# A GPTQ feed-forward behind a Mamba scan: the zero-subtracted integers of gate and up are unpacked a second time, after the scan

## The chip, the cores and the metric

The kernel runs on one core of one Trainium2 chip. The core has TensorE (PE; its weight loads are shown as PEld), VectorE (DVE), ScalarE (ACT), GpSimd (POOL) and SyncE (SP), which here only issues DMA transfers. The transfers run on 16 DMA engines. The metric is the device time of one execution in microseconds (us), taken as the median of some runs. The profile comes from one execution that was recorded by the hardware profiler.

## The reference

Two layers work on a state `x` of 2 batches, 512 tokens and 512 channels. Each of the four blocks is `x = x + layernorm(block(layernorm(x)))`. The first block is a Mamba block with a state of 16 per channel. The second, which the change is about, is a gated feed-forward with 4-bit GPTQ weights:

```python
def dequant_gptq(qweight, scales, zeros, groupsize):     # 8 nibbles along K in each int32
    q = qweight[k // PACK, :] >> (k % PACK * 4)[:, None] & 15
    z = zeros[:, n // PACK] >> (n % PACK * 4)[None, :] & 15
    s = scales.astype(jnp.float32)
    zp = (z.astype(jnp.float32) + 1.0) * s
    return q.astype(jnp.float32) * s[g] - zp[g]          # g = k // 128
...
gate = x2 @ Wg        # 512 -> 1376
up = x2 @ Wu          # 512 -> 1376
inter = gate * jax.nn.sigmoid(gate) * up
out = (inter @ Wd).astype(jnp.float16)
```

The third block is a small attention over 16 head channels, the fourth a feed-forward with a router; neither is touched.

## The kernel before

**Two forms of the same weights.** Gate and up have 512 rows and 1376 columns each. A packed word of a row of `gate_q` or `up_q` holds eight rows of the weight. One *word step* takes nibble `j` of every word of a stretch of columns, for gate and up at once (128 partitions: 64 of each), and gives 128 rows by up to 512 columns. There are three stretches (`CUTS`): 512, 512 and 352 columns, so 24 steps in all. Two results of a step are stored in DRAM: the integer less its zero point, `q - (z + 1)`, in `wgi_d`, and the same times the scale in `wgu_d`. Batch 0 multiplies with the scaled weights (`gu_weights(0, j)` reads `wgu_d`). Batch 1 multiplies with the integers (`gu_weights(1, j)` reads `wgi_d`), with its activations split into a high and a low part (`hhl`), and applies the scales (`gus`) as it takes the sums out of PSUM.

**A step in detail** (`GateUpWords.steps`, L278 to L315). `nibble` (L237, DVE) shifts and masks into a buffer `q`. Then the zero is subtracted into the same buffer, seen as float (`wi`): by DVE in one instruction (L292), or, where the step is given to GpSimd, by an ACT copy (L295) and a GpSimd subtraction (L299). SP stores `wi` to `wgi_d` (L303). GpSimd multiplies `wi` with the scale into another buffer `w` (L307), and stores that to `wgu_d` (L312; on GpSimd's queue in the head, on SP's in the scan). There are four buffers `q` and four `w` in the head, and four tiles of another pool stand in for `w` in the last four steps there. The integers' store walks the DRAM tensor in the order of its 4 groups of rows, then 32 rows in each:

```python
nc.sync.dma_start(
    out=wgi_d[j * RG : (j + 1) * RG, :, :, n0:n1].rearrange("r a k n -> k r a n"),
    in_=wi[:, :n],
)
```

**The stages.** *The head* (to 85.3 us, where the first scan instruction starts): batch 0 is normalised and transposed, then eight channel tiles of the Mamba input are projected (PE, `px`, L626), taken out with a bias (`evict_x`, ACT, L479), convolved (`conv`, three DVE instructions, L486) and put through `silu` (ACT, L640); two channels later their rank projection runs (PE, `psm`, L500). The word steps of the first two stretches are written between these channels: four at channel 0, then one per channel on DVE, two more on GpSimd's route at channel 2 and one more at channels 4 and 6, and the sixteenth after the ranks. After the ranks come their norm (`ranks_norm`, L507), a transpose (`pt`, L540), `dt`, and the loads of the broadcast rows B and C (L561). *The scan* (85.3 to 589 us) runs 128 steps of DVE multiply, DVE scan (L1108), GpSimd multiply (L1114) and PE sum (L1136), with the projections of batch 1 and batch 0's gate and up as side work; the eight steps of the third stretch are placed there (`words_job`, L1065). *Behind the scan* (590 to 659 us) PE does batch 1's Mamba output (`po`, L1309) and batch 0's down projection (`fo`, L1328), while `down_words` unpacks the down weights (DVE, GpSimd, SP) and `normed_job` normalises and transposes batch 1 (`tp_f`, L1285) into `hhl`. *Batch 1's gate, up and down* (`gptq(1)`, 659 to 755 us) follow: PE's `fg`, `fu` (L1450), taken out by ACT (L1432), DVE (L1436) and GpSimd (L1440), beside batch 0's attention. The rest (755 us on) is batch 1's attention and the last block.

**What sets the order.** Instructions of PE, ACT, DVE and GpSimd stand on their engines in the order in which they are traced (`pin`, L407). Side work is made of generators: `spawn` starts one after a lag, each `yield n` lets n ticks pass, and behind the scan there is one tick for each `po` or `fo` matmul of the source. DMA issues on SP are not pinned; they stand in an order that the tile scheduler decides, and SP works through them one by one, so an issue that waits for its data or its buffer holds up the issues behind it. Weights of gate, up, `wo` and `wd0` share three buffers (`wst`).

Of the kernel before, what the change touches and what calls it, by code (L numbers as in the profile page):

```python
# [57 lines left out]
def tile_sandwich(  # L58
# [157 lines left out]
    def word_loads(parts, n0, n1, qw, z, s, step, eng, engz):  # L216

        def at(p0, m):
            return slice(p0, p0 + step * (m - 1) + 1, step)

        n = n1 - n0
        for p0, src, r0, r1, sc, zd in parts:
            eng.dma_start(out=qw[at(p0, r1 - r0), :n], in_=src[r0:r1, n0:n1])
        for rows_, dst, en in ((4, s, eng), (5, z, engz)):
            for part in parts:
                p0, r0, r1, rows = part[0], part[2], part[3], part[rows_]
                g0, g1 = r0 // RG, r1 // RG
                for ga, gb, m in ((g0, g1, RG), (g1, g1 + 1, r1 - g1 * RG)):
                    if m:
                        q0 = p0 + step * (ga * RG - r0)  # L230
                        en.dma_start(
                            out=dst[at(q0, (gb - ga) * m), :n],
                            in_=rows[ga:gb, n0:n1].unsqueeze(1).to_broadcast([gb - ga, m, n]),
                        )
# [4 lines left out]
    class GateUpWords:  # L239
# [38 lines left out]
        def steps(self, eng=nc.vector):  # L278
            n0, n1, qw, z, s, q_, w_, j = self.todo.pop(0)
            n, nm = n1 - n0, f"gu{n0}_{j}"  # L280
            q = q_(nm)
            beside = bool(scans)
            if beside:
                eng = nc.gpsimd

            while beside and (now[0] % 2 == 0 or pool_at[0] == (now[0] - 1) // 2 - 1):
                yield 1
            nibble(q[:, :n], qw[:, :n], j)
            yield 2
            w, wi = w_(nm), q.bitcast(F32)  # L290
            if eng is nc.vector:
                eng.tensor_sub(wi[:, :n], q[:, :n], z[:, :n])  # L292
                yield 2
            else:
                nc.scalar.copy(wi[:, :n], q[:, :n])  # L295
                yield 2
                if beside:
                    yield from pool_turn()
                eng.tensor_sub(wi[:, :n], wi[:, :n], z[:, :n])  # L299
                yield 1  # L300
                if beside:
                    yield from pool_turn()
            nc.sync.dma_start(  # L303
                out=wgi_d[j * RG : (j + 1) * RG, :, :, n0:n1].rearrange("r a k n -> k r a n"),
                in_=wi[:, :n],
            )
            nc.gpsimd.tensor_mul(w[:, :n], wi[:, :n], s[:, :n])  # L307
            if beside:
                yield 2
            hp_ = KH * RG  # L310
            rows = slice(j % 2 * hp_, (j % 2 + 1) * hp_)
            (nc.sync if beside else nc.gpsimd).dma_start(  # L312
                out=wgu_d[rows, :, j // 2, n0:n1].rearrange("r a n -> (r a) n"), in_=w[:, :n]
            )
            yield 2  # L315
# [20 lines left out]
    def down_words(d, dq, loaded):  # L336

        nr = INTER // PACK
        m, hw = nr - P, H // 2
        qw, z, s, r, n = loaded  # L340
        wd_v = wd_d.rearrange("(r e) n -> e r n", e=PACK)
        for j in range(PACK):
            q = dq.tile([P, S], I32, tag="q", name=f"q_d{d}_{j}", bufs=2)
            nibble(q[:r, :n], qw[:r, :n], j)
            w = dq.tile([P, S], F32, tag="w", name=f"w_d{d}_{j}", bufs=3)
            nc.vector.tensor_sub(w[:r, :n], q[:r, :n], z[:r, :n])
            nc.gpsimd.tensor_mul(w[:r, :n], w[:r, :n], s[:r, :n])
            if d == 0:
                nc.sync.dma_start(out=wd_v[j, :P, :], in_=w[:, :H])
            else:  # L350
                for a in range(2):
                    nc.sync.dma_start(out=wd_v[j, P:nr, ts(a, hw)], in_=w[a * m : (a + 1) * m, :hw])
            yield 2 - j % 2

    def head_sums(dq):

# [71 lines left out]
    with ExitStack() as mamba:  # L428
# [786 lines left out]
        ps_x = pool(ctx, "px", 1, PSUM)  # L1215
        ps_tp = pool(ctx, "ptp", 1, PSUM)
        hlp = pool(ctx, "hl", side="right")
        hhl = [hlp.tile([P, KH, S], F32R, name=f"h{nm}1") for nm in ("hi", "lo")]

        def obank(name):  # L1220
# [30 lines left out]
        with ExitStack() as p3:  # L1251
            dq = pool(p3, "dq2", 1)

            def normed_job(i, ps):

                name = f"mo1_{i}"
                o = new_u(f"o1_{i}")
                nc.scalar.copy(o, ps)
                yield 3
                mv = moments([o], name)  # L1260
                rs = rstd(mv, name, 1)
                yield 2
                nm = minus_mean(mv, rs, name, 1)
                yield 1
                apply(o, o, rs, nm, 0)
                yield 2
                nc.vector.tensor_add(xs(1)[i], xs(1)[i], o)
                name = f"f1_{i}"
                mv = moments([xs(1)[i]], name)
                rs = rstd(mv, name, 1)  # L1270
                yield 2
                nm = minus_mean(mv, rs, name, 1)
                yield 1
                xn = jrow(f"xn_{name}")
                apply(
                    xn.rearrange("p (k j r) -> p k r j", k=KH, j=PACK),
                    xs(1)[i].rearrange("p (k r j) -> p k r j", k=KH, j=PACK), rs, nm, 0,
                )
                yield 2
                tps = []  # L1280

                def turn():
                    tp = bank(f"tp_f1_{i}").rearrange("p (k t) -> p k t", k=KH)
                    for kc in range(KH):
                        nc.tensor.transpose(tp[:, kc, :], xn[:, ts(kc, P)], ident)  # L1285
                    tps.append(tp)

                def split():
                    hi, lo = (t_[:, :, ts(i, P)] for t_ in hhl)
                    nc.scalar.copy(hi, tps[0])  # L1290
                    yield 1
                    nc.vector.tensor_sub(lo, tps[0], hi.bitcast(F32))

                asks.append((turn, split()))

            def words_jobs():
                yield from down_words(0, dq, down[0])
                yield from down_words(1, dq, down[1])
                yield 20
                yield from head_sums(dq)  # L1300

            def outs():
                po = [obank(f"po1_{i}") for i in range(TB)]
                for j in range(NCH // 2):
                    w = wo_pair(1, 0, j)
                    tiles = [(e, i) for e in range(2) for i in range(TB)]
                    for e, i in sorted(tiles, key=lambda ei: ei[j == NCH // 2 - 1]):
                        c = 2 * j + e
                        nc.tensor.matmul(  # L1309
                            po[i], g[1][c][:, ts(i, P)], w[:, e, :],  # L1310
                            start=(c == 0), stop=(c == NCH - 1),
                        )
                        yield
                        if c == NCH - 1:
                            spawn(normed_job(i, po[i]), 1)
                for i, m in enumerate(IC):
                    j, e = divmod(i, 2)
                    if not e:
                        w = wst.tile([P, 2, H], F32, tag="w4", name=f"wd0_{j}")
                        n = len(IC[i : i + 2])  # L1320
                        nc.sync.dma_start(
                            out=w[:m, :n],
                            in_=wd_d[i * P : i * P + n * m].rearrange("(k p) h -> p k h", p=m),
                        )
                    for t in range(TB):
                        if not i:
                            fo0.append(obank(f"fo0_{t}"))
                        nc.tensor.matmul(  # L1328
                            fo0[t], its[i][:m, ts(t, P)], w[:m, e],
                            start=(i == 0), stop=(i == len(IC) - 1),  # L1330
                        )
                        yield

            fo0 = []
            spawn(words_jobs(), 1)
            run(outs())
            while jobs or asks:
                if asks:
                    answer()
                tick()  # L1340
            pin()
# [304 lines left out]
    def chain(b, fo, ask):  # L1646
        yield from ffn_out(b, fo)
        yield from gptq_norm(b)
        yield from attention(b, ask)

    spawn(chain(0, fo0, lambda fn, then: asks.append((fn, then))), 1)
    run(gptq(1))
    while jobs or asks:
# [77 lines left out]
```

## Time and profile before

| | us |
|---|---|
| median of 3 runs | 925.68 (923.48 to 926.89) |
| the profiled execution | 925.2 |
| its span, first to last instruction | 923.4 |
| PE busy, whole span | 834.6 (90%) |
| DVE busy | 714.0 (77%) |
| POOL busy | 506.4 (55%) |
| ACT busy | 443.9 (48%) |

By stage (busy us of each engine, granted TensorE clock as a share of full speed, and the mean busy share of the 16 DMA engines):

| stage, us | PE | DVE | ACT | POOL | clock | DMA |
|---|---|---|---|---|---|---|
| head, 0 to 85.3 | 60.7 | 45.6 | 29.5 | 46.4 | 0.88 | 0.54 |
| scan, 85.3 to 589.9 | 457.8 | 482.4 | 315.1 | 389.6 | 0.96 | 0.25 |
| behind the scan, 589.9 to 659.1 | 69.2 | 36.6 | 13.1 | 20.5 | 0.97 | 0.52 |
| batch 1 gate, up, down, 659.1 to 755 | 91.2 | 72.4 | 54.3 | 33.8 | 1.00 | 0.30 |
| rest, 755 to 923.4 | 155.8 | 77.1 | 31.9 | 16.3 | 0.96 | 0.10 |

An engine that is busy for nearly all of a stage bounds it; where none is, the stage waits for something else, and the views of waits and of the timeline tell for what. The times of the stages are read off the first scan instruction, the first `po` and the first `fg` matmul. A busy PE is not PE at its peak, and matmul ends are modelled. Time in which an engine only issues a DMA is not counted as busy.

### The profile page before, as it was taken

Reading aid. Unit: us, or ns where it says so; the run is one execution under the profiler, and the core shown is the slowest. Engines: PE = TensorE matmul, PEld = TensorE weight load, DVE = VectorE, ACT = ScalarE, POOL = GpSimd, SP = SyncE. Lnnn points to the kernel's source line nnn. Section 1 sums busy time; section 2 is a strip of 40 time slices with the busy share of each in tenths; the row PEclk is TensorE's granted clock in tenths of the full one; section 3 lists DMA queues with packets and bytes.
Section 4 is the critical chain, followed back from the end, with each engine's and each line's share of the span. In section 5 each row is a group of like instructions: output and inputs, shape, how many; then the busy total and the mean of one; then the engine's idle time right before and its main releaser. Section 6 shows DMA issues by size and latency. Waiting matters only on the chain. (4 is left out here: it accounts for less than half of the span.)

```text
span 923.4 us, 7390 instructions
## 1 busy us (share of the span) xinstructions
PE 834.6 (90%) x2188; PEld 386.6 (42%) x2188; DVE 714.0 (77%) x835; ACT 443.9 (48%) x682; POOL 506.4 (55%) x354
## 2 busy tenths in 40 slices
PE   6678897987999989959999999799989999999995
PEld 3343333332354434324444443244446545545442
DVE  6545999999999999999999999665385964445226
ACT  3226787566567755564656555013345554310110
POOL 6642988776688778886778787541133420011001
PEclk9887999998999999999999999799999999999998
DMA  6654911111000494410110102364332231101001
GB/s 190 215 192 157 361 60 33 47 46 54 23 24 26 131 330 169 160 41 0 46 45 23 46 9 85 127 222 160 91 92 69 71 115 55 59 12 57 24 0 46
DMA packets 47130, 85.76 MB, mean 93 GB/s; under 512 B 8014, under 2 KB 22201, under 8 KB 47090
## 3 DMA queue, kind: packets, MB, share of 16 engines
q1 hardware_dynamic: 44818, 79.29, 25.5%
q0 software_dynamic: 1984, 5.47, 1.7%
q10 hardware_dynamic: 288, 0.52, 0.2%
q8 instruction: 17, 0.28, 0.1%
q14 instruction: 23, 0.19, 0.1%
HBM read 68.40 MB, written 16.88 MB: 92 GB/s over the span
## 5 line engine op out<-in xcount | busy, mean ns | idle before, releaser
L1114 POOL TENSOR_TENSOR bx<-bx,C 128x1024 f32<-128x1024 f32 x128 | 302.0, 2360 | 107.3 <-DVE bx L1108 79.7
L1108 DVE TENSOR_TENSOR_SCAN bx<-da,bx 128x1024 f32<-128x1024 f32 x128 | 291.5, 2278 | 0.0
L1136 PE MATMUL py<-bx,ident 128*128 128x512 f32 x480 | 236.5, 623 | 28.1 <-POOL bx L1114 24.4
L1088 ACT ACTIVATE da<-dt,A 128x511 f32<-128x511 f32 x256 | 176.6, 691 | 144.0 <-DVE bx L1108 139.1
L1104 DVE TENSOR_TENSOR bx<-du,B 128x1024 f32<-128x1024 f32 x127 | 152.9, 1204 | 5.2 <-ACT da L1088 2.8
L1136 PEld LDWEIGHTS py<-bx,ident 128*128 128x128 f32 x480 | 92.0, 198 | 154.8 <-issue 96.7
L130 POOL TENSOR_TENSOR rs_lo<-ve_lo,mhalf 128x1 f32<-128x1 f32 x8 | 7.0, 880 | 91.8 <-DVE ve_lo L128 91.8
L756 PE MATMUL pg<-xT,w_g 128*128 128x512 f32 x114 | 55.7, 619 | 1.1 <-ACT dt L574 1.1
L1571 PE MATMUL pup<-hT_l,wup 128*128 128x512 f32 x128 | 56.2, 593 | 0.0
L1635 PE MATMUL pd<-wdn,hid 128*128 128x512 f32 x128 | 55.6, 595 | 0.0
L1440 POOL TENSOR_TENSOR pg<-pg,pg 128x512 f32<-128x512 f32 (+1 forms) x11 | 15.3, 1391 | 59.0 <-DVE pg L1436 59.0
L1411 PE MATMUL fo<-wd,pg 128*128 128x512 f32 (+1 forms) x88 | 44.2, 593 | 0.1
L1028 PE MATMUL fg<-hT_f,wg 128*128 128x512 f32 (+1 forms) x88 | 42.5, 594 | 0.0
L1028 PE MATMUL fu<-hT_f,wu 128*128 128x512 f32 (+1 forms) x88 | 40.4, 594 | 1.4 <-ACT dt L574 1.4
L486 DVE SCALAR_TENSOR_TENSOR u<-px,ch,u 128x511 f32<-128x511 f32 (+2 forms) x48 | 35.8, 747 | 7.0 <-ACT u L479 5.9
L1328 PE MATMUL fo<-wd,it 128*128 128x512 f32 (+1 forms) x88 | 38.6, 592 | 0.0
L1635 PEld LDWEIGHTS pd<-wdn,hid 128*128 128x128 f32 x128 | 24.6, 192 | 31.4 <-issue 30.9
L1571 PEld LDWEIGHTS pup<-hT_l,wup 128*128 128x128 f32 x128 | 23.9, 190 | 28.2 <-issue 28.2
L1588 DVE TENSOR_TENSOR hid<-hid 128x512 f32<-128x512 f32 x16 | 11.0, 687 | 32.0 <-ACT hid L1587 32.0
L756 PEld LDWEIGHTS pg<-xT,w_g 128*128 128x128 f32 x114 | 22.1, 198 | 31.6 <-issue 28.4
L626 PE MATMUL px<-xT,w_x 128*128 128x512 f32 x64 | 33.3, 671 | 0.7 <-ACT xT L606 0.7
L1436 DVE SCALAR_TENSOR_TENSOR pg<-fg,gus,pg 128x512 f32<-128x512 f32 (+1 forms) x22 | 16.3, 742 | 21.0 <-ACT pg L1432 21.0
(253 smaller groups left out, 1262.8 us busy)
## 6 DMA issues: line engine op xcount, KB each, us to landing
wo<-in_W_outT SPq DMA_DIRECT2D x20, 512.0 KB
B<-scr SPq DMA_DIRECT2D x16, 512.0 KB
C<-scr SPq DMA_DIRECT2D x16, 512.0 KB
w_x<-in_W_in SPq DMA_DIRECT2D x8, 512.0 KB
wgi_d<-q_gu SPq DMA_DIRECT2D x16, 256.0 KB
wgu_d<-w_gu POOLq DMA_DIRECT2D x16, 256.0 KB, 6.2
w_g<-in_W_in SPq DMA_DIRECT2D x8, 512.0 KB
wup<-in_up_w SPq DMA_DIRECT2D x8, 512.0 KB
```

What stands on the lines that cost most here:

```text
L486: nc.vector.scalar_tensor_tensor(uc[:, s:], ps[:, : S - s], ch[:, c, KCONV - 1 - s : KCONV - s], uc[:, s:], ALU.mult, ALU.add,)
L756: nc.tensor.matmul(ps, w[:, k, ts(e, P)], xT[b][:, k, :], start=(k == 0), stop=(k == KH - 1))
L1028: nc.tensor.matmul(ps[:m], wt[j][a][:, kc, e * P : e * P + m], hT[:, kc, :], start=(kc == 0), stop=(kc == KH - 1),)
L1088: nc.scalar.activation(das[s % 2][:, i, 1:], st["dt", b, c][:, 1:], AF.Exp, scale=A[:, c, n : n + 1])
L1104: nc.vector.tensor_mul(bx, st["du"].unsqueeze(1).to_broadcast([P, NG, S]), Bbs[b][gi])
L1108: nc.vector.tensor_tensor_scan(flat, das[s % 2].rearrange("p n t -> p (n t)"), flat, 0.0, ALU.mult, ALU.add)
L1114: nc.gpsimd.tensor_mul(bxs[s], bxs[s], Cbs[b][s % NGI])
L1136: nc.tensor.matmul(st["y"], ident, bx[:, i, :], start=False, stop=last)
L1328: nc.tensor.matmul(fo0[t], its[i][:m, ts(t, P)], w[:m, e], start=(i == 0), stop=(i == len(IC) - 1),)
L1411: nc.tensor.matmul(fo[t], its[i][:m, ts(t, P)], w[:m], start=(i == 0), stop=(i == len(IC) - 1),)
L1571: nc.tensor.matmul(ps, w[:, kc, ts(e, P)], src[kc], start=(kc == 0), stop=(kc == KH - 1))
L1635: nc.tensor.matmul(pd, hid[kc][:, ts(i, P)], wdn[kc], start=(kc == 0), stop=(kc == INT // P - 1),)
```

## The change

A step in the head or the scan no longer stores the integers: the subtraction (on either route) writes the buffer `w` instead of `q`, the multiplication works in place on `w`, and only `wgu_d` is stored. New generators (`whole_words`) load the packed words and the zeros of each stretch once more, without the scales, and make the integers again: nibble on DVE, copy on ACT, subtraction on GpSimd in place, and the store to `wgi_d` from SP, with three buffers `q` of their own. They use memory that held B and C. The first two stretches (16 steps) are spawned behind the scan with a lag of 24 ticks, three ticks a step; the third (8 steps) runs beside batch 1's gate and up.

```diff
@@ word_loads
         for rows_, dst, en in ((4, s, eng), (5, z, engz)):
+            if dst is None:
+                continue
@@ GateUpWords.steps
             nibble(q[:, :n], qw[:, :n], j)
             yield 2
-            w, wi = w_(nm), q.bitcast(F32)
+            w = w_(nm)
             if eng is nc.vector:
-                eng.tensor_sub(wi[:, :n], q[:, :n], z[:, :n])
+                eng.tensor_sub(w[:, :n], q[:, :n], z[:, :n])
                 yield 2
             else:
-                nc.scalar.copy(wi[:, :n], q[:, :n])
+                nc.scalar.copy(w[:, :n], q[:, :n])
                 yield 2
                 if beside:
                     yield from pool_turn()
-                eng.tensor_sub(wi[:, :n], wi[:, :n], z[:, :n])
+                eng.tensor_sub(w[:, :n], w[:, :n], z[:, :n])
                 yield 1
                 if beside:
                     yield from pool_turn()
-            nc.sync.dma_start(
-                out=wgi_d[j * RG : (j + 1) * RG, :, :, n0:n1].rearrange("r a k n -> k r a n"),
-                in_=wi[:, :n],
-            )
-            nc.gpsimd.tensor_mul(w[:, :n], wi[:, :n], s[:, :n])
+            nc.gpsimd.tensor_mul(w[:, :n], w[:, :n], s[:, :n])
@@ new
+    def whole_words(a, iq):
+        n0, n1 = CUTS[a][0] * PW, min(CUTS[a][1] * PW, INTER)
+        n = n1 - n0
+        qw = iq.tile([P, CW], I32, tag=f"qw{a}", name=f"qw_w{a}")
+        z = iq.tile([P, CW], F16, tag=f"z{a}", name=f"z_w{a}")
+        parts = [(i, src, 0, KH * RG, None, zd) for i, (src, zd) in enumerate(zip((gate_q, up_q), zds))]
+        word_loads(parts, n0, n1, qw, z, None, 2, nc.sync, nc.sync)
+        def words():
+            for j in range(PACK):
+                q = iq.tile([P, CW], I32, tag="q", name=f"q_w{a}_{j}", bufs=3)
+                nibble(q[:, :n], qw[:, :n], j)
+                yield 1
+                w = q.bitcast(F32)
+                nc.scalar.copy(w[:, :n], q[:, :n])
+                yield 1
+                nc.gpsimd.tensor_sub(w[:, :n], w[:, :n], z[:, :n])
+                nc.sync.dma_start(
+                    out=wgi_d[j * RG : (j + 1) * RG, :, :, n0:n1].rearrange("r a k n -> k r a n"),
+                    in_=w[:, :n],
+                )
+                yield 1
+        return words()
@@ behind the scan
+        iqp = pool(ctx, "iq", side="right")
...
+            def whole_jobs():
+                for words in whole[:2]:
+                    yield from words
+
+            whole = [whole_words(a, iqp) for a in range(len(CUTS))]
             fo0 = []
             spawn(words_jobs(), 1)
+            spawn(whole_jobs(), 24)
             run(outs())
@@ batch 1's gate and up
+    spawn(whole[2], 2)
     spawn(chain(0, fo0, lambda fn, then: asks.append((fn, then))), 1)
     run(gptq(1))
```

The order in which SP's instructions stand after the change: the 12 loads of words and zeros come behind the load of `wo` for the third pair and ahead of the first store of the down weights; the 16 stores of integers come from the last store of the down weights on, one by one between the loads of `wd0`, `wd1`, `wq`, `down_w`, gamma and beta, the last of them directly ahead of the first load of batch 1's gate (`wg1_0`). On PE the order is unchanged; on ACT, DVE and GpSimd the new instructions stand between those of `normed_job`, `head_sums` and batch 1's gate and up.

## The prediction

> **What bounds the kernel now.** I read first the table of waits, cut to 12 to 100 us (the head and the start of the scan): engine, line, what it waited for, us in total, times, longest.
>
> ```profile
> PEld psm L500 <- ACT u L640: 20.0, 5, 8.8
> ...
> DVE q_gu L237 <- DMA wgi_d<-q_gu: 16.2, 5, 5.2
> ```
>
> TensorE's longest wait is for `silu` on `u` (L640). That waits for VectorE's `conv` (L486), and VectorE stands in the line below: a nibble may not overwrite its `q` buffer until the integers in it have been written to `wgi_d`. The timeline of VectorE shows the place:
>
> ```profile
> 28.52 2.32 DVE L486 SCALAR_TENSOR_TENSOR u<-px,ch,u 128x511 f32<-128x511 f32 x3 [0.29 <-ACT u L479]
> ...
> 37.10 0.43 DVE L237 TENSOR_SCALAR q_gu<-qw_gu 128x512 int32<-128x512 int32 x1 [5.20 <-DMA wgi_d<-q_gu]
> ...
> 42.29 2.31 DVE L486 SCALAR_TENSOR_TENSOR u<-px,ch,u 128x511 f32<-128x511 f32 x3 [1.36 <-ACT u L479]
> ```
>
> Channels 2 and 3 start their `conv` 13.8 us apart; where nothing waits, 42.29 to 46.02 for instance, it is 3.7. In windows of 5 us (PE busy, PEld, DVE, ACT, POOL, then granted clock, DMA share, GB/s) TensorE falls idle and its clock to half:
>
> ```profile
> 40.00:45.00 5.00, 0.00 (x0) 0.00 (x0) 3.53 (x6) 1.60 (x3) 4.19 (x5) 0.59 0.45 165
> 45.00:50.00 5.00, 4.62 (x12) 3.07 (x13) 3.09 (x5) 1.62 (x3) 1.78 (x3) 0.50 0.67 233
> ```
>
> Why is a `wgi_d` write so slow? Its last two columns are plain where it is alone, in the scan (issue at 153.85; 176 KB, then at 158.0 the `wgu_d` write of the same bytes):
>
> ```profile
> 155.00:155.50 0.50, 1.00 0.23 34
> 155.50:156.00 0.50, 1.00 0.22 39
> 156.00:156.50 0.50, 1.00 0.28 101
> 156.50:157.00 0.50, 1.00 0.27 101
> ...
> 158.00:158.50 0.50, 1.00 0.82 301
> ```
>
> The integers hold about a quarter of the 16 DMA engines (0.22 to 0.28) for 3 us and end at 101 GB/s; the scaled weights hold 0.82 of them for half a microsecond. So a full `wgi_d` write (256 KB) costs four engines 262,144 B / 101 GB/s = 2.6 us. A transfer over all engines has a share on those four too and queues behind it, which the issues show: an `x` load, 0.4 us at the start, takes SP 3.87 us here.
>
> ```profile
> 34.66 0.52 SPq L303 DMA_DIRECT2D wgi_d<-q_gu  x1
> 35.23 3.87 SPq L84 DMA_DIRECT2D x<-in_x_in  x1
> ```
>
> The buffer written from 34.66 is free at 49.82 (VectorE's wait there ends), 15 us later. The head is thus bound by these four engines: 15 writes by 2.6 = 39 us of the 53 between 19.3 and 72, the rest their share of everything else. The scan (85.3 to 585) is bound by VectorE, 462.5 us busy of the 480 from 120 to 600. Behind it the chain of waits (start, us, what) is TensorE without a gap:
>
> ```profile
> 589.94 29.65 PE po L1309 x64
> ...
> 636.80 22.32 PE fo L1328 x52
> 659.12 0.48 PE fg L1450 x2
> ```
>
> and from 659 on VectorE again:
>
> ```profile
> 665.00:670.00 5.00, 4.18 (x14) 2.23 (x14) 4.86 (x14) 3.51 (x5) 2.90 (x3) 1.00 0.36 105
> ```
>
> **Part 1, the head (a gain).** Sixteen `wgi_d` writes leave, 15 of them ahead of the rank matmuls' end. The order on PE, ACT, DVE and POOL is unchanged there, so the stalls simply close up. From `conv` 2 (28.52) to `conv` 7 (68.81) are five channels and 40.3 us. New pace, from rows: a channel with a VectorE word takes 3.7; a GpSimd word adds a nibble, its ACT copy and the wait behind them (54.15 to 55.95 is 1.80 from nibble to `conv`, against 0.3): 5.2; two of them (channel 2) 5.8. Sum 5.8 + 3.7 + 5.2 + 3.7 + 5.2 = 23.6, above TensorE's own 4.32 a channel (29.41 to 33.73) by 5 = 21.6. Gain 16.7. Behind it TensorE holds its clock: the six L665 matmuls take 5.17 us at 0.65 and would take 2.6 at full, so `pt` no longer waits for them: 2.5. The write of the last word (L303 at 81.82), ahead of the loads of B and C, goes: 0.3 to 2.6, I take 0.3. Together 19.5.
>
> A wait takes the place of the one removed: the subtraction now writes `w` (four buffers), so VectorE or ACT, not GpSimd, waits until `wgu_d` has the word four back, with `conv` or the next `evict_x` queued behind. These writes land in 5.6 to 9.2 us, median 6.2. Word 6's copy (about 32.3) needs word 2's write (issued 25.45, landed 31.7): free; word 7's (32.9) needs 27.51 + 6.2 = 33.7: 0.8 late; the later ones come out within 1 us, and four tiles are apart. At 9.2 each it would be some 8 us. Bounds of part 1: 12 (that), and 23 (TensorE's pace, all of the last write).
>
> **Part 2, the scan.** Eight smaller writes leave SP. VectorE does not wait for them: nothing. The cover is its 0.96 busy share.
>
> **Part 3, behind the scan (a loss).** Loads of packed words and zeros: 12 DMAs, free to go by 580, when SP idles until 589; nothing. Then 16 words: nibble 0.42, ACT copy 0.62, GpSimd subtraction 1.15, an SP issue of 0.52: 7, 10, 18 and 8 us in all, beside engines that are 53%, 19% and 30% busy in this stage. That work is hidden. The writes are not. The first nibbles stand behind the last word of `down_words` (DVE, 616.4), so the first write goes at about 619.6. From there SP's order has, up to the first load that batch 1 needs (`wg1_0`), 16 writes of 256 KB with 6.2 MB of other transfers between (`wd0`, `wd1`, `wq`, `down_w`, gamma, beta, `wg1_0` itself). On the four engines: 16 by 2.6 = 41.6, and 6.2 MB at the 370 GB/s of full share = 16.7. Sum 58.3: `wg1_0` has moved at 678, plus 2.0 to land (3.4 from issue to landing on the chain at 687, less 1.4 of moving) = 680. TensorE wants it at 659.1. Loss 21. Three `q` buffers give no bubble: a word is ready 2.5 us after its buffer is free, and two more writes are queued. On the way TensorE waits for `wd0_4` and `wd0_5`, which SP issues behind words 9 and 12, and for a normalised tile of batch 1 behind words 4 and 5 (DVE and ACT have these in between); these waits end before 680 and lie inside the 21. Bounds: the head's own rate (55 us less 20 of other transfers, over 15 writes, 2.3 each) gives 14; other transfers at 320 GB/s and all landings in line give 25.
>
> The row says a quarter of the engines. [...]
>
> **Part 4, batch 1's gate and up (a loss).** Eight words of 352 columns fall where VectorE is 97% busy: 8 by 0.35 = 2.8 (a nibble takes 0.28 at 256 columns, 0.42 at 512; the copies and subtractions fall into idle time of ACT and GpSimd); TensorE starts at half clock after its wait, as at 585 to 595 (0.50, 0.61): 2; `wu1_1` lies behind two writes of 1.8 us with 2 to 3 of slack: 0.2. Together 5, bounds 0 (all in slack) and 10 (each late load felt).
>
> **Sum.** The profiled execution took 925.2 (span 923.4), 0.5 below the median of 925.68: 925.2 - 19.5 + 21 + 5 = 931.7, so 932. Own range: 925.2 - 23 + 14 = 916 to 925.2 - 12 + 25 + 10 = 948.
>
> **Rivals.** *The writes are hidden.* From 640 to 655 VectorE, ACT and GpSimd are idle and the DMA share is 0.02 to 0.35. If 16 writes cost what `wgu_d` costs (262 KB at 301 GB/s, 0.9 us), they need 14 + 17 = 31 us of 39 and end by 651; only the words' delay of the first transposes stays, 2: 925.2 - 19.5 + 2 + 4 = 912. Against: the 0.25 share. It decides between 0.9 and 1.4 us a write (16 by 1.4 + 17 = 39). This is the other side.
> *Both sides cancel.* Parts 1 and 3 at 21 and 15, part 4 at 4: 923. For: each is the same engines' time, freed in one place and taken in another; here they have 15 us of idle behind the scan to take.
> *The head keeps its stalls*, in the `wgu_d` waits: gain 10, 941. Against: GpSimd waited for them 2.3 us in all.
> *The stores do not leave the head*: excluded, SP's order has none there.
>
> **How the numbers follow.** Forecast 0.52, cancel 0.22, hidden 0.18, head 0.08. Half a percent, 4.6 us, is what can be told from no change: faster 0.19 (hidden, and a rest), same 0.23, slower 0.58. Range 914 to 946: it takes in cancelling, and leaves hidden and the far end of the losses outside.
>
> **What would show it.** First scan instruction near 66 instead of 85.3; no wait of L237 on `wgi_d` in the head; granted clock there near 1. After the scan a DMA share of 0.25 to 0.6 up to the end, the chain with a DMA in front of `fg` and TensorE idle for some 20 us around it. Wrong if `fg` starts 69 us after `po` as now (659.12 less 589.94), or if the first scan comes later than 75.

## The result, and the profile after

The changed kernel takes 935.36 us (median of 4 runs, 933.81 to 937.26), the kernel before 925.62; the ratio is 1.0109, with a 95% interval of 1.0082 to 1.0135. It is slower, as forecast, 3.4 us above the predicted time. The profiled execution's span went from 923.4 to 932.0.

Both signs that the prediction named are there. First the head, in the table of waits from 10 to 75 us (engine, line, what it waited for, us in total, times, longest):

```profile
ACT u L664 <- DVE u L510: 19.0, 7, 4.1
PEld px L650 <- issue: 13.0, 50, 0.5
PEld psm L524 <- ACT u L664: 9.4, 6, 1.8
POOL w_gu L305 <- DVE w_gu L294: 7.4, 7, 2.7
```

No row of a nibble waiting for `wgi_d` is left, and TensorE's longest wait for `u` is 1.8 us where it was 8.8. VectorE's timeline has `conv` of channels 2 and 7 (L510 here) at

```profile
28.17 2.32 DVE L510 SCALAR_TENSOR_TENSOR u<-px,ch,u 128x511 f32<-128x511 f32 x3 [0.23 <-ACT u L503]
...
54.31 2.31 DVE L510 SCALAR_TENSOR_TENSOR u<-px,ch,u 128x511 f32<-128x511 f32 x3 [1.37 <-ACT u L503]
```

26.1 us apart (40.3 before), and the windows that showed an idle TensorE at half clock show a busy one at full clock:

```profile
40.00:45.00 5.00, 4.15 (x16) 2.14 (x15) 3.77 (x7) 1.62 (x3) 3.53 (x4) 1.00 0.57 211
45.00:50.00 5.00, 4.34 (x17) 2.28 (x16) 4.48 (x6) 1.61 (x3) 4.08 (x5) 1.00 0.20 77
```

The first scan starts at 67.5 us in place of 85.3. Behind the scan it is the other way round. TensorE's table of waits from 595 to 680 us, where the kernel before has no wait of TensorE over 1 us up to `fg`:

```profile
PE fg L1481 <- DMA wg<-wgi_d: 10.9, 1, 10.9
PE fo L1353 <- DMA wd<-wd_d: 5.2, 2, 3.7
PE tp_f L1310 <- ACT xn_f L153: 3.3, 1, 3.3
PE fo L1353 <- ACT o L1283: 1.8, 1, 1.8
```

The chain of waits that ended last shows what the first of them hangs on (start, us, what): a write of integers that takes 7.8 us to land, the nibble that waited for its buffer, its copy and subtraction, an SP issue, and the load behind it.

```profile
641.53 7.82 DMA wgi_d<-q_w
649.44 0.44 DVE q_w L239
649.90 0.62 ACT q_w L368
650.60 1.16 POOL q_w L370
651.77 0.53 SPq L371
652.41 8.58 DMA wg<-wgi_d
661.12 2.91 PE fg L1481 x6
```

And the DMA part of the page, cut to 620 to 662 us (40 slices of 1.05 us: busy share of the 16 engines in tenths, GB/s), shows how slow the writes are: for long stretches the share is 2 tenths and the rate 98 to 101 GB/s. In windows of 1 us at 98 to 102 GB/s the share is 0.26 to 0.28 (623 to 624 or 646 to 647 us, for instance), about what four engines of the 16 would give.

```profile
DMA  4942632593227322227822752222694299999222
GB/s 146 365 160 101 257 129 99 162 371 139 99 99 236 135 92 98 80 74 211 302 84 98 189 199 99 99 80 101 197 304 168 100 229 379 389 284 326 98 90 70
```

By stages of the two profiled executions (first `scan`, first `po`, first `fg`, last `fu`, end):

| stage | before | after | difference |
|---|---|---|---|
| start to first scan | 85.3 | 67.5 | -17.8 |
| first scan to last scan | 495.2 | 492.9 | -2.3 |
| last scan to `po` to first `fo` | 9.4 + 29.5 | 7.9 + 27.5 | -3.5 |
| first `fo` to first `fg` | 39.2 | 65.3 | +26.1 |
| first `fg` to last `fu` | 86.9 | 91.3 | +4.4 |
| last `fu` to the end | 177.9 | 179.6 | +1.7 |
| span | 923.4 | 932.0 | +8.6 |

### The profile page after: what moved, and what is told of

The parts are those of the page before. It is cut to its first block, busy times and chain, and to the rows that moved or that the text cites. A ratio compares the mean times of both kernels' runs of the same rounds, so it can differ in the third digit from the quotient of the medians.

```text
span 932.0 us, 7483 instructions
## 1 busy us (share of the span) xinstructions
PE 828.5 (89%) x2188; PEld 383.7 (41%) x2188; DVE 729.6 (78%) x859; ACT 455.7 (49%) x706; POOL 535.6 (57%) x378
## 5 line engine op out<-in xcount | busy, mean ns | idle before, releaser
L1160 PE MATMUL py<-bx,ident 128*128 128x512 f32 x480 | 232.2, 613 | 27.4 <-POOL bx L1138 23.6
L1160 PEld LDWEIGHTS py<-bx,ident 128*128 128x128 f32 x480 | 91.3, 196 | 151.1 <-issue 96.4
L368 ACT CAST q_w<-q_w 128x512 f32<-128x512 int32 (+1 forms) x24 | 13.7, 572 | 76.3 <-DVE q_w L239 75.2
L1353 PE MATMUL fo<-wd,it 128*128 128x512 f32 (+1 forms) x88 | 42.8, 639 | 7.0 <-DMA wd<-wd_d 5.2
L370 POOL TENSOR_TENSOR q_w<-q_w,z_w 128x512 f32<-128x512 f32 (+1 forms) x24 | 26.3, 1096 | 39.1 <-ACT q_w L368 36.2
L510 DVE SCALAR_TENSOR_TENSOR u<-px,ch,u 128x511 f32<-128x511 f32 (+2 forms) x48 | 35.9, 747 | 6.5 <-ACT u L503 5.4
L1481 PE MATMUL fg<-hhi,wg 128*128 128x512 f32 (+1 forms) x44 | 24.1, 549 | 13.7 <-DMA wg<-wgi_d 10.9
```

The costliest lines, as they stand in the source:

```text
L1160: nc.tensor.matmul(st["y"], ident, bx[:, i, :], start=False, stop=last)
L1353: nc.tensor.matmul(fo0[t], its[i][:m, ts(t, P)], w[:m, e], start=(i == 0), stop=(i == len(IC) - 1),)
L1481: nc.tensor.matmul(ps[:m], w[:, k, e * P : e * P + m].bitcast(F32R), part[:, k, :], start=(n == 0), stop=(n == 1),)
```

## The experiments

Times are medians beside the kernel before on the same chip, which took 921.1 to 923.5 us there; ratios are the measure across the three groups of runs (the first two rows are of a fourth group, where the kernel before took 925.6). "po to fg" and "fg to fu" are stages of the profiled execution.

| kernel | us | ratio, interval | first scan | po to fg | fg to fu |
|---|---|---|---|---|---|
| before | 925.6 | 1 | 85.3 | 68.7 | 86.9 |
| after | 935.4 | 1.0109 [1.0082, 1.0135] | 67.5 | 92.8 | 91.3 |
| a_spread | 914.5 | 0.9919 [0.9893, 0.9945] | 68.2 | 73.1 | 90.0 |
| b_spread | 901.4 | 0.9773 [0.9731, 0.9814] | 69.2 | 66.9 | 88.6 |
| a_nostore | 912.0 | 0.9892 [0.9850, 0.9933] | 68.3 | 73.6 | 91.7 |
| b_nostore | 906.1 | 0.9821 [0.9790, 0.9851] | 69.2 | 66.7 | 87.0 |
| a_q6 | 934.6 | 1.0144 [1.0109, 1.0179] | 68.4 | 95.3 | 90.8 |
| a_third_scan | 934.7 | 1.0151 [1.0115, 1.0186] | 68.0 | 96.8 | 88.2 |
| a_early | 938.2 | 1.0193 [1.0140, 1.0247] | 67.9 | 98.7 | 90.0 |
| b_split4 | 916.8 | 0.9961 [0.9939, 0.9982] | 83.5 | 66.7 | 87.0 |
| a_split2 | 973.7 | 1.0551 [1.0496, 1.0606] | 69.3 | 133.1 | 92.5 |
| a_split4 | 927.1 | 1.0053 [1.0023, 1.0083] | 68.9 | 89.4 | 90.5 |
| a_nowords | 906.2 | 0.9815 [0.9785, 0.9844] | 68.3 | 66.7 | 86.9 |

The expected times below were worked out from the 925.6 and 935.4 of the first two rows. Taken by ratio (ratio times 925.6), `a_spread`, `a_nostore`, `b_nostore`, `a_q6` and `a_nowords` stand up to 1 us above the ranges that their medians lie in, and `b_spread`, whose median of 901.4 is just under its range, lies inside at 904.6. The stages are the firmer half of each test.

**The same words, the same places, 128 rows outermost.** `a_spread` keeps everything of the kernel after but the order of the 128 partitions, so that a word's rows lie on the DRAM side as one dimension of 128.

```diff
-    wgi_d = dram.tile([P, 2, KH, INTER], F32, tag="wgi", name="wgi_d")
+    wgi_d = dram.tile([P, KH, 2, INTER], F32, tag="wgi", name="wgi_d")
...
-            eng.dma_start(out=qw[at(p0, r1 - r0), :n], in_=src[r0:r1, n0:n1])
+            words_ = src[r0:r1, n0:n1].rearrange("(k r) n -> r k n", k=KH)
+            eng.dma_start(out=qw[at(p0, r1 - r0), :n], in_=words_)
-                            in_=rows[ga:gb, n0:n1].unsqueeze(1).to_broadcast([gb - ga, m, n]),
+                            in_=rows[ga:gb, n0:n1].unsqueeze(0).to_broadcast([m, gb - ga, n]),
...
-  out=wgi_d[j * RG : (j + 1) * RG, :, :, n0:n1].rearrange("r a k n -> k r a n"),
+  out=wgi_d[j * RG : (j + 1) * RG, :, :, n0:n1].rearrange("r k a n -> (r k a) n"),
-  w4(src[:, a, :, cols], ...)
+  w4(src[:, :, a, cols] if b else src[:, a, :, cols], ...)
```

> The kernel after, with the same 24 words in the same places; only the partition order of the integers is changed to (row, chunk, gate/up) and that of wgi_d to [128, 4, 2, 1376], so that the write of a word has one outermost dimension of 128 rows on the DRAM side in place of one of 4. Theory (four DMA engines): a write of 262 KB then costs about 0.9 us of all 16 engines, as a wgu_d write does (301 GB/s), in place of 2.6 us of four. The load of wg1_0 comes before TensorE wants it, fg starts 69 to 73 us after po (92.8 in the kernel after), no wait of L239 on wgi_d over 2 us in all; time 935.4 - 22 = 913 (909 to 918). Rival 1 (the words themselves: nibbles, copies and subtractions stand ahead of the normalised tiles of batch 1 in the queues of VectorE, ScalarE and GpSimd): fg stays 85 or more after po, time over 928. Rival 2 (bytes: 4.2 MB more in a stretch that is short of transfer time): time over 925.

914.5 us, inside the theory's range (918.1 by ratio, at its edge); `fg` comes 73.1 us after `po`, where the first rival had 85 or more, and the second rival's 925 is out by 10 us, or 7 by ratio. In TensorE's table the wait of `fg` for `wg` is 1.1 us and no wait of `fo` for `wd` is left. VectorE's waits for `wgi_d`, expected under 2 us in all, are 3.4 from 590 to 650 us. The loads of packed words and zeros take the new order too (the first lines of the diff, for these words only). The same 4.2 MB behind the scan cost almost nothing in this order (the DMA share in windows of 5 us from 605 to 645 us is 0.54 to 0.94, in the kernel after 0.36 to 0.72): `fg` comes no later than in `a_nostore` below, which writes nothing (73.6).

**The same in the place of the kernel before.** `b_spread` makes that change in the head and the scan. The scaled weights come from the same words, so the normalised rows of batch 0 take the new order too:

```diff
-                    xn.rearrange("p (k a r) -> p r k a", k=KH, a=2),
-                    xs(b)[i].rearrange("p (r k a) -> p r k a", k=KH, a=2), rs, nm, 0,
+                    xn.rearrange("p (e r q) -> p q r e", e=PACK, q=KH),
+                    xs(b)[i].rearrange("p (q r e) -> p q r e", e=PACK, q=KH), rs, nm, 0,
```

> The kernel before, nothing moved: 24 words in the head and the scan, each with both stores; only the partition order of the words (and with it that of the normalised rows of batch 0, which the scaled weights meet) and the layout of wgi_d are changed, so that each wgi_d write spreads over 16 engines. Theory (four DMA engines): the stalls of the head close as in the kernel after (first scan instruction at 67 to 71 us; 85.3 before, 67.5 after), and nothing comes behind the scan (fg 69 us after po): time 925.6 - 19 = 906 (902 to 912). Rival (the head stalls because a q buffer has to wait for a store at all, whatever the store's shape): first scan later than 78, time over 918.

901.4 us, 2.3% under the kernel before (1.9 to 2.7) and the fastest of all: it has the head of the kernel after and, to within 2 us, the stages behind the scan of the kernel before. Its write of integers alone in the scan, issued at 135.35 us, in windows whose last two columns are DMA share and GB/s, to be laid beside the four rows of 155 to 157 us in the prediction:

```profile
135.50:136.00 0.50, 0.50 (x4) 0.29 (x4) 0.50 (x2) 0.19 (x1) 0.50 (x1) 1.00 0.00 0
136.00:136.50 0.50, 0.36 (x4) 0.12 (x2) 0.50 (x1) 0.50 (x2) 0.50 (x1) 1.00 0.61 231
136.50:137.00 0.50, 0.00 (x0) 0.00 (x0) 0.50 (x1) 0.49 (x1) 0.50 (x1) 1.00 0.36 130
137.00:137.50 0.50, 0.46 (x1) 0.30 (x2) 0.50 (x1) 0.50 (x1) 0.50 (x1) 1.00 0.00 0
```

It is gone within a microsecond where it took three. The share reads 0.61 at most in these windows; the 16 engines of the expectation are not shown.

**Stores left out.** `a_nostore` and `b_nostore` drop the `dma_start` to `wgi_d` in either place:

```diff
-            nc.sync.dma_start(
-                out=wgi_d[j * RG : (j + 1) * RG, :, :, n0:n1].rearrange("r a k n -> k r a n"),
-                in_=w[:, :n],
-            )
-        src = wgi_d if b else wgu_d
+        src = wgu_d
```

> The kernel after with the 24 nibbles, copies and subtractions of the second extraction, but without their stores to wgi_d; the gate and up of batch 1 load the scaled weights of wgu_d instead, so that the second output is that of other weights. Theory: the whole loss behind the scan is the stores', fg 69 to 72 after po, time 935.4 - 24 = 911 (907 to 915); what is left above b_nostore (about 4 to 8 us) is the 24 words' work on VectorE, ScalarE and GpSimd. Rival 1 (the words themselves): over 925.

> The kernel before with all words, but without the stores of their integers to wgi_d; the gate and up of batch 1 load the scaled weights of wgu_d instead, so that the second output is that of other weights. Theory: the head's gain in the kernel after comes from these stores alone: first scan at 66 to 69, all later stages keep their lengths, time 925.6 - 20 = 905 (901 to 909). Rival (part of the head's gain is that the subtraction writes w, so that q buffers are free earlier): first scan later than 72, time over 910.

912.0 and 906.1 us. Without the stores the old head is as short as the new one (first scan 69.2; the kernels with the new head lie between 67.5 and 69.3): the head's gain comes from leaving the stores out, and none that shows comes from the subtraction's new buffer. And without the stores behind the scan the ratio falls from 1.0109 to 0.9892, some 20 us: they are nearly the whole loss. (`b_spread`, which stores everything, reads 4.7 us under `b_nostore`. The intervals overlap and the two profiles are 1.9 us apart; why it isn't slower stays open.) What remains above `b_nostore` is other work, and TensorE's weight loads between 598 and 662 us of `a_nostore` show where it sits:

```profile
PEld fo L1349 <- ACT o L1279: 4.8, 4, 2.7
PEld fg L1477 <- DVE pu L1463: 3.0, 4, 1.2
PEld tp_f L1306 <- ACT xn_f L153: 2.6, 4, 1.2
```

The first `fo` waits for ScalarE's copies of `po` into `o` (4.8 us in four waits); these copies, and the normalisation of the rows of batch 1 behind them (`xn_f`), stand in the queues between the copies and nibbles of words.

**Without the second extraction.** `a_nowords` takes these words out too, as a control:

```diff
-            whole = [whole_words(a, iqp) for a in range(len(CUTS))]
-            spawn(whole_jobs(), 24)
-    spawn(whole[2], 2)
```

> The kernel after without the second extraction altogether (no loads of words and zeros, no nibbles, copies, subtractions and stores behind the scan); the gate and up of batch 1 load the scaled weights of wgu_d instead, so that the second output is that of other weights. Theory: what a_nostore still loses against b_nostore (912.0 against 906.1) is the work of the 24 words on VectorE, ScalarE and GpSimd: without it fg comes 68 to 70 after po, first fg to last fu takes 87 to 88.5, time 905 (902 to 908). Rival (the loss lies in another order of the other instructions behind the scan, or in chance): 909 or more.

906.2 us, `po` to `fg` 66.7, `fg` to `fu` 86.9: the same as `b_nostore`. So the words' instructions, without any write, cost some 6 us by the times (912.0 and 906.2, from two groups of runs) and 7 by the ratios (0.9892 and 0.9815), and what is left of the kernel after is the kernel before without stores.

**Half the engines.** The strongest test of the theory makes each write smaller and, if it holds, slower: two DMAs of two chunks each.

```diff
-                nc.sync.dma_start(
-                    out=wgi_d[j * RG : (j + 1) * RG, :, :, n0:n1].rearrange("r a k n -> k r a n"),
-                    in_=w[:, :n],
-                )
+                for k in range(0, KH, 2):
+                    nc.sync.dma_start(
+                        out=wgi_d[j * RG : (j + 1) * RG, :, k : k + 2, n0:n1].rearrange("r a k n -> k r a n"),
+                        in_=w[k * 2 * RG : (k + 2) * 2 * RG, :n],
+                    )
```

> The kernel after, but each wgi_d write of the second extraction is issued as two DMAs of two chunks each, half the bytes a piece, with an outermost dimension of 2 on the DRAM side; layout, partition order and the order of all other instructions stay. Theory (the outermost dimension sets the number of engines, and a queue always begins at the same one): both halves hold the same two engines, a word's write takes twice as long, about 5.2 us of two engines; between the bursts the DMA share is about 0.12 and 50 GB/s, the loss behind the scan grows by 30 to 45 us: time 965 to 985. Rival (each DMA gets engines of its own, or smaller DMAs simply run beside each other): the halves share the load over four or more engines, time under 945.

973.7 us, in the middle of the theory's range. The DMA rows of this kernel from 620 to 700 us (40 slices of 2 us):

```profile
DMA  4931271111331111141291111111141111111287
GB/s 115 365 128 57 75 251 51 49 49 50 83 130 49 49 49 50 73 140 49 70 335 57 42 28 45 49 49 49 49 164 49 49 49 50 49 49 49 59 267 206
```

One tenth and 49 GB/s, slice after slice: 0.13 in the window from 650 to 651 us, about what two engines of the 16 would give. A word has two halves of 2.7 us each at that rate, and up to seven slices of 2 us in a row stay at 49 to 50 GB/s, so that the halves together move no faster than one: the same two engines, by this estimate. `po` to `fg` grows by 133.1 - 92.8 = 40.3 us over 16 writes, 2.5 us a write. SP's order did not stay, against the expectation: the load of `wg1_0` stands behind all 16 as before, but ten loads of 256 KB (three of `wd1`, five of `down_w`, gamma and beta) that stood ahead of it stand behind it now, 2.6 MB or some 7 us at 370 GB/s (the fullest slices of the kernel after, in the rows further up, read 365 to 389). So 2.5 us is not the price of a write alone, and that it comes so near the expected 2.6 is partly luck; the rate in the rows is shown.

**Four DMAs a word.** `a_split4` and `b_split4` have the old layout and issue a write by chunk, 32 rows each:

```diff
+            for k in range(KH):
+                nc.sync.dma_start(
+                    out=wgi_d[j * RG : (j + 1) * RG, :, k, n0:n1].rearrange("r a n -> (r a) n"),
+                    in_=wi[k * 2 * RG : (k + 1) * 2 * RG, :n],
+                )
```

> The kernel before with its layout and partition order as they are; only each wgi_d write is issued as four DMAs of 32 partitions, whose slowest dimension on the DRAM side is 32 rows in place of 4 chunks. Theory (spread over the engines, not layout): the head closes up as in b_spread, first scan at 68 to 72 us, time 901 to 910; 3 more issues of SP for each of 24 words are hidden by its idle time. Rival (it was the new partition order and layout that made b_spread fast): first scan over 80, time over 918.

> The kernel after, but each wgi_d write of the second extraction is issued as four DMAs of one chunk each, with 32 rows as the slowest dimension on the DRAM side; layout, partition order and the order of all other instructions stay. Theory (spread over the engines): as a_spread, fg 72 to 77 after po, time 914 to 920; the 72 additional issues of SP (0.3 to 0.5 us each, some 29 us, 22 of them ahead of wg1_0) go into its idle time. Rival (the new layout and partition order made a_spread fast, or the issues fill SP): over 926.

916.8 and 927.1 us: both miss, and `b_split4`'s head stays long (first scan 83.5). Yet its table of VectorE's waits from 10 to 84 us has no wait of a nibble for `wgi_d` any more. Its SP timeline and TensorE's waits there say what took its place:

```profile
19.51 33.91 SPq L304 DMA_DIRECT2D wgi_d<-q_gu  x48
53.52 0.38 SPq L114 DMA_DIRECT2D w_x<-in_W_in  x1
```

```profile
PEld px L627 <- DMA w_x<-in_W_in: 15.2, 1, 15.2
PE px L627 <- DMA w_x<-in_W_in: 14.4, 1, 14.4
```

48 issues, those of twelve words, stand in SP's program ahead of the fourth load of `w_x`, which stood behind two words' writes before: more instructions of a kind changed the order in which SP's program was laid out, and SP waits in that order for words that are not made yet. `a_split4` has the same, against its expectation, in which the order was to stay: 28 issues in a row from 597.6 to 620.1 us ahead of `wq` and the third load of `wd0`, and TensorE waits 13.2 us for `wd`. So the times of these two don't tell spread from layout. The rows do: `a_split2`, which changed neither layout nor partition order, shows half the share at half the rate, and a word of `b_split4` that is alone in the scan (four issues from 151.61 us, 176 KB together) shows a share of 0.38, 0.45 and 0.37 in the half microseconds from 152.5 on, where one write of the old shape held 0.22 to 0.28. With the old layout and 32 rows outermost the pieces together hold more than four engines (0.37 to 0.45 of 16 is 6 to 7); the word takes about 2 us, over the 1.70 us that SP needs for its four issues.

**More buffers.** `a_q6` has six `q` buffers in place of three.

```diff
-                q = iq.tile([P, CW], I32, tag="q", name=f"q_w{a}_{j}", bufs=3)
+                q = iq.tile([P, CW], I32, tag="q", name=f"q_w{a}_{j}", bufs=6)
```

> The kernel after with six q buffers for the words of the second extraction in place of three; nothing else. Theory (the four engines are never without a write, as the rows at 0.22 and 98 GB/s between 620 and 650 us say): VectorE's 23.5 us of waits of L239 on wgi_d go, the writes are issued earlier and queue longer, and wg1_0 lands no earlier: fg 90 to 94 us after po (92.8 in the kernel after), time 935 (931 to 938). Rival (three buffers leave bubbles: each word waits some 8 us for its landing, so three in flight set the pace): six shorten it, fg 80 or less after po, time under 925.

934.6 us, no gain. (The share beside 98 GB/s is 0.26 or 0.27 in windows of 1 us, not 0.22.) VectorE's waits for `wgi_d` fall from 23.5 to 5.6 us, and TensorE waits elsewhere instead. Its waits from 566 to 680 us:

```profile
PE fo L1353 <- DMA wd<-wd_d: 18.3, 2, 16.1
PE fo L1353 <- ACT o L1283: 2.2, 1, 2.2
```

The writes issued earlier only stand earlier in front of the `wd0` loads; that a part of each load has to pass the engines that the writes hold is an estimate, since no view tells the engines apart.

**An earlier start.** `a_early` starts the 16 words between the down words.

```diff
-            spawn(whole_jobs(), 24)
+            spawn(whole_jobs(), 1)
```

> The kernel after with the 16 words of the first two stretches started with the down words and between them, 14 us earlier (a lag of 1 instead of 24 steps). Theory (16 writes in a row on four engines, whose end sets fg): the writes start some 20 us earlier and so does their end, fg 72 to 80 after po, time 915 to 924; what stays shows as a wait of fo on wd, since the down words now stand behind words that wait for their buffers. Rival (not the writes' number and pace but their place beside the other loads decides): fg 88 or more after po, time over 930.

938.2 us: the theory's numbers were wrong, the rival's hold. The first write goes at 572.1 us and the last at 642.5 (596.3 and 651.8 in the kernel after): 24 us earlier at one end, 9 at the other. But the down words, which share VectorE and SP with them, end at 608, and TensorE's waits from 566 to 680 us are

```profile
PE fo L1353 <- DMA wd<-wd_d: 29.4, 1, 29.4
PE fg L1481 <- DVE pu L1467: 1.2, 2, 0.8
```

One wait of 29.4 us ahead of the first `fo`, none ahead of `fg`. The expectation had the wait of `fo` as a rest; it was the whole. What counts is thus not when the writes end but what stands behind them in the queues.

**The third stretch back in the scan.** `a_third_scan` extracts only 16 words again; the last 8 keep both stores in the scan, with `wi = q.bitcast(F32)` and the store of the kernel before for that stretch, and `whole_words` for the first two.

> The kernel after, but the third stretch of columns (8 words of 352) keeps both stores in the scan, as in the kernel before; only 16 words are extracted again. Theory: the loss between fg and the last fu (91.3 us from the first fg to the last fu; 86.9 in the kernel before) is these 8 words' instructions on VectorE, ScalarE and GpSimd and their writes: it shrinks to 88 or less, fg stays 90 to 94 after po, time 935.4 - 4 = 931 (928 to 934). Rival (the loss there comes of the late start itself, loads and clock): still 90 or more, time over 934.

`fg` to `fu` takes 88.2 us (91.3), as expected, so these 8 words are about 3 us of that stage. The time does not follow: 934.7 us, a ratio of 1.0151 against 1.0109 with intervals that overlap. In this execution `fg` came 4.0 us later after `po`, 1.9 of them in `po` itself (29.4 from `po` to `fo` in place of 27.5). The 1.9 belong to the half clock of the last section; the other 2 stay open.

## Why the prediction was right, step by step

**Which engines the write holds, and its price.** Right. 2.6 us a write on four engines was read from a lone write and the share beside it. Halving the share added about 2.5 us a write, with fewer other loads in front, where the price says 2.6; the write with 128 rows outermost brought `fg` back from 92.8 to 73.1 us after `po`. The number of engines is an estimate from the shares. Windows in which nothing else moves read 0.27 and 99 to 101 GB/s where the slowest dimension on the DRAM side is 4 (the kernel before, 134.5 to 135.5 us), 0.13 and 49 GB/s where it is 2 (`a_split2`, 650 to 651 us), and in the fullest window 0.61 and 231 GB/s where it is 128 (`b_spread`, 136 to 136.5 us).

**Part 1, the head.** Forecast 19.5, measured 17.8. The pace was the over-estimate: conv 2 to conv 7 takes 26.1 us where the sum over rows gave 23.6, so 14.2 in place of 16.7. Most of that is one channel: from conv 3 (34.65) to conv 4 (40.11) it takes 5.46 us where the sum had 3.7, with a nibble of 1.74 and a subtraction of 1.47 us on VectorE that take 0.42 and 0.69 elsewhere; why, the runs don't show. The feared `wgu_d` waits didn't come: no row of VectorE, ScalarE or GpSimd in the head waits for a write to `wgu_d`. What was put behind it (2.5 + 0.3) is 3.3: from conv 7 to the first scan it takes 13.2 us where it took 16.5. (The 0.65 that the prediction puts beside the six L665 matmuls is the row of 75 to 80 us; over the matmuls themselves, 73.6 to 79, the granted clock was 0.55.) `b_nostore` shows that the stores alone make this gain.

**Part 2, the scan.** Forecast nothing, measured 2.3 us less from first to last scan. The profiles of the kernels with a short head lie between 490 and 495 us there, so a part of it is chance of one execution. A further 3.5 us came between the last scan and the first `fo`, which no term had; it is in the last section.

**Part 3, behind the scan.** Forecast 21, measured 26.1 without those 3.5. The path was the forecast one: the writes on their four engines, the load of `wg1_0` behind them, and TensorE waiting for it. Two readings of the 5 us that the sum missed stand side by side. By leaving the stores out: `a_nostore` takes 44.1 us from `fo` to `fg` in place of 39.2, so the words' instructions alone cost 4.9, and the writes add 21.2 to that. There "That work is hidden" failed: 18 us of GpSimd, 10 of ScalarE and 7 of VectorE do fit beside engines that are 19% to 53% busy over the stage, but not at the moment where they stand. ScalarE's copy of a word stands ahead of a copy into `o` that TensorE wants at once, and so with the nibbles. A mean share of busy time covers nothing that stands in line ahead of an urgent instruction.

Along the path that set `fg` in the kernel after it looks different. The sum had the first write at 619.6 us and `wg1_0` landed at 680, 60.4 us; it took from 596.3 to 661.0, 64.7 us. TensorE stood idle for the last 10.9 of them, so what ScalarE's copies had cost it before was covered there. The 4.3 us that the sum has too little lie in the transfers, their landing, or a word's own instructions between them, which the runs don't separate. So the two costs don't simply add, and that 21.2 comes so near the forecast 21 doesn't show that the writes' term was right to a tenth: along the path it was some 4 us too small.

"Three `q` buffers give no bubble" was right (`a_q6`). That the waits for `wd0` and for normalised tiles end before the load of `wg1_0` and lie inside the loss held as well: TensorE waited for `wd` in `after`, and still 10.9 us for `wg` behind it.

**Part 4.** Forecast 5, measured 6.1: 4.4 from `fg` to `fu`, which `a_nostore` against `a_nowords` (91.7 and 86.9) gives to the words. The half clock that the sum put at 2 was there (0.50 until 664 us), but costs nothing that shows: `a_nostore` came into this stage at full clock and took 91.7 against 91.3. The words, put at 2.8, cost 3 to 5: the profiles with all eight of them lie between 90.0 and 92.5, those without between 86.9 and 88.6. The 1.7 behind it lies inside what these profiles differ by there (176.0 to 180.3).

So 925.2 - 17.8 - 2.3 - 3.5 + 26.1 + 4.4 + 1.7 = 933.8, the time of the profiled execution. The forecast's 932 is near it partly by luck: the 5.1 that part 3 cost more, the 1.7 that the head gave less and the 1.1 of part 4 were mostly met by 5.8 that nobody had counted.

**The rivals.** "The writes are hidden" was wrong for this write and near for its condition: with a write that holds more engines (0.61 of them in `b_spread`) `a_spread` is 0.8% faster than the kernel before, some 7.5 us, where that rival had 13. "Both sides cancel" is out: it had 21 for part 1 and 15 for part 3, which are 17.8 and 26.1; the idle 15 us behind the scan did not take up the difference.

## What to carry to other kernels

When a transfer is slow, look at the DMA share beside its GB/s before moving it. Here 101 GB/s stood beside a share of 0.27, where the fullest slices read 389 GB/s, and the mending was a partition order and a layout with 128 rows as the slowest dimension (231 GB/s beside 0.61), not another place. Moving the transfer took the wait along; it cost more in the new place (26.1 us up to `fg`) than it freed in the old (17.8), and with the pattern mended the old place was the best of all (901.4 us). Smaller pieces were no cure by themselves: two halves moved at half the rate (49 GB/s), and four pieces of 32 rows changed the order of the issuing queue.

## What the runs showed of the hardware

Between the last scan and `fo` the profiles fall into two groups that no edit separates. TensorE's timeline of the kernel before, then of the kernel after (start, us, instructions in one stretch, idle time before them):

```profile
582.23 2.44 PE L1136 MATMUL py<-bx,ident 128*128 128x512 f32 x4 [2.39 <-POOL bx L1114]
585.33 3.78 PE L1136 MATMUL py<-bx,ident 128*128 128x512 f32 x4 [0.67 <-POOL bx L1114]
589.94 10.34 PE L1309 MATMUL po<-wo,g 128*128 128x512 f32 x19 [0.82 <-issue]
```

```profile
562.14 5.32 PE L1160 MATMUL py<-bx,ident 128*128 128x512 f32 x8 [2.40 <-POOL bx L1138]
568.29 12.25 PE L1334 MATMUL po<-wo,g 128*128 128x512 f32 x28 [0.83 <-issue]
```

Behind the same idle 2.4 us the eight `py` matmuls take 2.44 and 3.78 us in the kernel before and 5.32 in the kernel after, and the `po` matmuls start at 0.54 us each in the one and 0.44 in the other; the granted clock was 0.50 and 0.61 in the kernel before (585 to 595 us) and 0.70, 0.96 and 1.00 in the kernel after (560 to 575). `a_nostore`, `a_third_scan` and `a_split2` go with the kernel before, the other profiles with the kernel after. It is worth 3.5 us.

Windows of half a microsecond show more. The clock falls to 0.50 in both kernels; what differs is how long it stays there. Estimated from these windows, the first and the last of them counted in part, it is 10.2 us in the kernel before, `a_nostore`, `a_third_scan` and `a_split2`, and 3.4 us, a third of that, in the other profiles, but for `b_split4`, whose clock doesn't fall at all. The long stretches are those that begin latest: 1.2 to 1.4 us behind the start of the first `py` matmul after the wait (583.6 against 582.23 in the kernel before), the short ones at 1.1 us at most (562.0 against 562.14 in the kernel after). What sets the moment of the fall isn't shown.

An issue of the write with 128 rows outermost takes SP 0.32 us in the scan, one of the write of the kernel before 0.52 (b_spread at 135.35 us, before at 153.85), for the same 176 KB. And with four engines, or two, as the shares have it, 99 and 49 GB/s come to about 25 GB/s an engine, an estimate for these writes of 2 KB rows.
